# q as two float32r pieces in place of three bf16 pieces, with five record buffers in place of six

## The chip, the core and the metric

The kernel runs on one core of a Trainium2 chip. The core has five engines that run on their own instruction streams: PE (TensorE, matrix products; its weight loads are listed apart as PEld), DVE (VectorE), ACT (ScalarE), POOL (GpSimd) and SP (SyncE, which here only issues transfers). Transfers run on 16 DMA engines. The time is device time of one execution in microseconds, and lower is better. Three executions took 5041.39, 5045.82 and 5046.07 us, a median of 5045.82.

## What is computed

One graph-attention layer over 12,500 nodes with 128 features and 412,500 edges with 64 features, with a residual and two layer norms:

```python
h, q, k, v = x @ Wn + bn, x @ Wq + bq, x @ Wk + bk, x @ Wv + bv
attn_in = concatenate([q[src], k[tgt], edge @ We + be], axis=-1)
hmid = leaky_relu(attn_in @ A1 + b1, 0.2)
scores = leaky_relu(hmid @ A2 + b2, 0.2)
w = softmax(scores.mean(axis=-1), axis=0)          # over all edges
out = segment_sum(w[:, None] * v[tgt], src, num_nodes)
x = layernorm(x + gamma * norm(h + out) + beta)
```

The edges come sorted by tgt (dst). The first layer is linear in its three parts, so q and k already carry their part of A1: the hidden value of an edge is q'[src] + k'[dst] + e'.

## The kernel before

Nodes are laid out as 128 partitions times 98 blocks (nb). Edges come in 403 groups of 8 tiles of 128 edges, sorted by dst. The groups are cut into six parts (CUTS) of 51, 62, 73, 73, 73 and 71 groups.

**Production (`make`, lines 784 to 1009).** For each group, PE multiplies one-hots of dst with rows of the kv table and adds the edge term (`rows`, L901 and L907) into `pkv`; ACT copies two tiles by two into a record buffer `rec` and appends the local src (`evacuate`, L918 and L919); POOL sends each tile's 128 records with an indirect DMA to the place in `rtab` that belongs to the src block (L930). So each record buffer holds four tiles: one ACT copy writes it, four scatters read it, and it is free again when they have landed. `rp = pool("rec", 6)` at L746 has six of them. DVE makes the one-hots (L823, L844), the counts (L834) and the places (L870, L881).

**Sums (`sums_of`, lines 1027 to 1352).** A unit is two src blocks of one part, 49 units a part and 294 in all, each with 14 tiles (four parts), 12 or 10 tiles. A unit's steps are:

- `load` (L1064, SP) brings the unit's records into `rt`, 1820 KB for 14 tiles, and `load_q` (L1075) brings q's pieces of its blocks into `qs`;
- `sources` (L1086, DVE) takes the src column out of `rt`, `turn` (L1094, PE) and `turned` (L1101, DVE) transpose it, `put` (L1108, SP) writes the few bytes to DRAM as `row`, `spread` (L1113, SP) reads them back to all partitions as `rowB`;
- `onehot` (L1122, DVE) compares `rowB` with the partition number and gives `ohT`, for four tiles (512 columns) at a time;
- `hidden` (PE) transposes the k + e part of the four tiles into `ph` (L1133) and adds q of the edge's src by products of q's pieces with `ohT` (L1142), once for each piece;
- `sloped` (L1153, ACT) and `leaky` (L1157, DVE) make the leaky relu `hm`; `scores`, `above_zero` and `heads` give the score (L1170, L1184, L1196), `weights` its exponential (L1235);
- `select` (L1244, DVE) and `weigh` (L1258, ACT) make one-hots times weights, `add` (L1287, PE) sums the v part into `psm`, `total` (L1303, DVE) adds the parts so far, `store` (L1310, SP) writes them.

The steps of eight or so units overlap by a plan that is written out by hand (`do(step, ...)`, eight steps a unit of 14 tiles). At the end of `sorted_path` the loop over parts (from L1608) interleaves the production of part p with the sums of part p-1 in program order; every engine and SP's queue then work strictly in that order. The last part's sums follow after the last group, and `closing` adds the norms in 14 groups of seven blocks.

**Tables (`tables`, from L1535).** During the first part's production, 13 further chunks of the kv table and then 14 chunks of q and h are computed. `parts3` (L1523) cuts a float32 value into three bf16 pieces: a copy by ACT (L1526), a subtraction by DVE (L1531), a copy, a subtraction, a copy. The pieces of q go to `qtab` in DRAM (L1582).

What the code relies on in the products of L1142: a one-hot column picks one row of q, so each piece's product is exact, and three bf16 pieces added up give q back.

Of the kernel before, what the change touches and what calls it, by code (L numbers as in the profile page):

```python
# [9 lines left out]

FP = mybir.dt.float32
BF = mybir.dt.bfloat16
I32 = mybir.dt.int32
U8 = mybir.dt.uint8
AF = mybir.ActivationFunctionType
ALU = mybir.AluOpType
# [4 lines left out]
P = 128  # L21
D = 128
# [4 lines left out]
NB = 7  # L27
# [64 lines left out]
def general(  # L92
# [20 lines left out]

    srcI = const.tile([P, T], I32)
    nc.sync.dma_start(out=srcI, in_=src)

    nc.vector.tensor_scalar(srcI, srcI, rows - 1, None, op0=ALU.min)
    dstI = const.tile([P, T], I32)
    nc.sync.dma_start(out=dstI, in_=dst)
# [155 lines left out]
    with tc.tile_pool(name="gvg", bufs=3) as vp, tc.tile_pool(  # L275
# [7 lines left out]
        def front(g):  # L283
# [30 lines left out]
            )  # L314
            idx = ip.tile([P, GT], I32)
            nc.vector.tensor_tensor(idx, mv, srcF[:, cols], op=ALU.add)
# [136 lines left out]
def sorted_path(  # L453
# [8 lines left out]
    nc = tc.nc  # L462
    nb = plan.nb
# [4 lines left out]

    const = ctx.enter_context(tc.tile_pool(name="const", bufs=1))
    dram = ctx.enter_context(tc.tile_pool(name="dram", bufs=1, space=DRAM))  # L470
    qtab = dram.tile([P, nb, 3 * D], BF, name="qtab")
    kvtab = dram.tile([nb * P, 6 * D], BF, name="kvtab")
    htab = dram.tile([P, nb, D], FP, name="htab")
    xtab = dram.tile([P, nb, D], FP, name="xtab")
# [2 lines left out]
    dtab = dram.tile([G, EG], U8, name="dtab")  # L477
    stab = dram.tile([G, 1], I32, name="stab")

    ident = const.tile([P, P], FP)  # L480
    make_identity(nc, ident)
    identB = const.tile([P, P], BF)
    nc.vector.tensor_copy(identB, ident)
    iotaE = const.tile([P, P, 4], BF)
    nc.gpsimd.iota(iotaE, pattern=[[1, P], [0, 4]], base=0, channel_multiplier=0,
# [21 lines left out]
    for j, part in enumerate((1.0, -1.0)):  # L507
# [13 lines left out]
        out=signs, in_=signs, compare_op=ALU.not_equal, fill=SLOPE - 1, base=-(H + 2),  # L521
# [57 lines left out]
    pool = lambda name, bufs, **k: work.enter_context(tc.tile_pool(name=name, bufs=bufs, **k))  # L579
# [7 lines left out]
    def kv_product(xt, pool, j):  # L587
        pn = pool.tile([P, 4 * P], FP, name="ph")
        nc.tensor.matmul(
            pn[:, : 2 * D], xt[:, j, :], Wkv.rearrange("k s d -> k (s d)"), start=True, stop=True  # L590
        )
        return pn

    def kv_biased(ns, j, pn):
        nc.vector.tensor_add(
            ns[:, j, :, :], pn[:, : 2 * D].rearrange("p (s d) -> p s d", s=2), bias_kv
        )

    def kv_rows(c):

        return kvtab[c * NB * P : (c + 1) * NB * P, :].rearrange("(p b) w -> p (b w)", p=P)

    with tc.tile_pool(name="prep", bufs=1) as prep, tc.tile_pool(
        name="pprep", bufs=1, space=PSUM
# [8 lines left out]
        ns = prep.tile([P, NB, 2, D], FP, name="ns")  # L613
        for j in range(NB):
            kv_biased(ns, j, kv_product(xt, pnode, j))
        skv = prep.tile([P, NB, 3, 2, D], BF, name="skv")
        rest = ns
# [13 lines left out]
    nc.vector.memset(bad, -1.0)  # L631
    blk = const.tile([P, T], BF)
    srcl = const.tile([P, T], U8)
    twin = const.tile([P, T], U8)
    start = const.tile([1, G], I32)
    chunks = [(0, min(CH, G))] + [
# [5 lines left out]
    def edges(tmp, c, size):  # L642

        g0, g1 = chunks[c]
        m = g1 - g0
        dI = tmp.tile([size, EG], I32, name="dI")
        nc.sync.dma_start(out=dI[:m, :], in_=dst_g[g0:g1, :])
# [60 lines left out]
    def spans():  # L708
# [24 lines left out]
        out=above, in_=above, compare_op=ALU.is_gt, fill=0.0, base=0,  # L733
# [9 lines left out]
    kvp = pool("kvs", 5)  # L743
    lp = pool("plc", 2)
    ixp = pool("idx", 6)
    rp = pool("rec", 6)  # L746
    pkvp = pool("pkv", 1, space=PSUM)
    pcp = pool("pcn", 1, space=PSUM)

    qp = pool("qs", 3)  # L750
    slp = pool("sl", 7)
    rowp = pool("row", 2)
    op_ = pool("oht", 3)
# [273 lines left out]
    def sums_of(bp):  # L1027
# [43 lines left out]

        def load_q(i):
            bs = units[i][1]
            qs = qp.tile([P, 2, 3, D], BF, name="qs")
            nc.sync.dma_start(  # L1075
                out=qs[:, : len(bs), :, :].rearrange("p b s d -> p b (s d)"),
                in_=qtab[:, bs[0] : bs[-1] + 1, :],
            )
            state[i]["qs"] = qs
# [38 lines left out]

        def onehot(i, t0, n, k):
            st = state[i]  # L1120
            st["oh"][k] = op_.tile([P, 4 * P], BF, name="ohT")
            nc.vector.tensor_scalar(  # L1122
                st["oh"][k][:, : n * P], st["rowB"][:, t0 * P : (t0 + n) * P], iotaP, None,
                op0=ALU.is_equal,
            )


        def hidden(i, t0, c, n, k):
            st = state[i]
            oh = st["oh"].pop(k)  # L1130
            ph = php.tile([D, 4 * P], FP, name="ph")
            for j in range(n):
                nc.tensor.matmul(  # L1133
                    ph[:, j * P : (j + 1) * P], st["rt"][:, t0 + j, :D], ident,
                    is_transpose=True, start=(j == 0), stop=False,
                )
            t, j0 = units[i][2], t0
            while j0 < t0 + n:
                j1 = min(t0 + n, (j0 // t + 1) * t)
                cols = slice((j0 - t0) * P, (j1 - t0) * P)  # L1140
                for s in range(3):
                    nc.tensor.matmul(  # L1142
                        ph[:, cols], st["qs"][:, j0 // t, s, :], oh[:, cols], start=False,
                        stop=(s == 2 and j1 == t0 + n),
                    )
                j0 = j1
            if c == 0:
                st["hm"][t0 - c] = hp.tile([D, TM * P], FP, name="hm")
            st["ph", k] = ph
# [164 lines left out]
        for i, (nt, nk, s0, load_at, f, e, turn_at) in enumerate(plans):  # L1314
# [4 lines left out]
            do(s0 - turn_at + 1 + e, put, i)  # L1319
            do(s0 - turn_at + 3 + 2 * e, spread, i)  # L1320
            do(s0 - 9, load_q, i)
            for k in range(nk):
                c = 4 * k
                n, s = min(4, nt - c), s0 + 2 * k
# [14 lines left out]
            for j, t0 in enumerate(range(0, nt, 4)):  # L1339
                n = min(4, nt - t0)  # L1340
# [182 lines left out]
    def parts3(to, rest, half):  # L1523

        for s in range(3):
            nc.scalar.activation(to[s], rest, AF.Copy)  # L1526
            yield
            if s < 2:
                less = np_.tile([P, NB, 2, D], FP, name=f"less{s}")
                less = less[:, :, :half, :]  # L1530
                nc.vector.tensor_tensor(less, rest, to[s], op=ALU.subtract)  # L1531
                rest = less
                yield

    def tables():  # L1535
        jobs = [(True, c) for c in range(1, ng)] + [(False, g) for g in range(ng)]
        xts = {}

        def load_x(i):
            if i < len(jobs):  # L1540
                kv, g = jobs[i]
                xts[i] = xp.tile([D, NB, P], FP, name="xt")
                nc.sync.dma_start(
                    out=xts[i], in_=xN[:, g, :, :] if kv else xT[:, g * NB : (g + 1) * NB, :]
                )

        load_x(0)
        yield
        for i, (kv, g) in enumerate(jobs):
            load_x(i + 1)  # L1550
            xt = xts.pop(i)
            ns = np_.tile([P, NB, 2, D], FP, name=f"ns{i % 2}")
            w, bias = (Wkv, bias_kv) if kv else (Wqh, bias_qh)
            for j in range(NB + 1):
                before = ph if j else None
                if j < NB:
                    ph = php.tile([P, 4 * P], FP, name="ph")
                    nc.tensor.matmul(
                        ph[:, : 2 * D], xt[:, j, :], w.rearrange("k s d -> k (s d)"),
                        start=True, stop=True,  # L1560
                    )
                if j:
                    nc.vector.tensor_tensor(
                        ns[:, j - 1, :, :].rearrange("p s d -> p (s d)"), before[:, : 2 * D],
                        bias.rearrange("p s d -> p (s d)"), op=ALU.add,
                    )
                yield
            sp = np_.tile([P, NB, 3, 2, D], BF, name="sp")
            if kv:
                yield from parts3([sp[:, :, s, :, :] for s in range(3)], ns, 2)  # L1570
                nc.sync.dma_start(
                    out=kv_rows(g), in_=sp.rearrange("p b s t d -> p (b s t d)")
                )
                made_rows[0] = g + 1
            else:
                sq = sp.rearrange("p b s t d -> p (b s t d)")[:, : NB * 3 * D].rearrange(
                    "p (b s o d) -> p b s o d", b=NB, s=3, o=1
                )
                yield from parts3([sq[:, :, s, :, :] for s in range(3)], ns[:, :, 0:1, :], 1)
                bl = slice(g * NB, (g + 1) * NB)  # L1580
                nc.sync.dma_start(out=htab[:, bl, :], in_=ns[:, :, 1, :])
                nc.sync.dma_start(  # L1582
                    out=qtab[:, bl, :], in_=sq.rearrange("p b s o d -> p b (s o d)")
                )
            yield
# [147 lines left out]
```

## Time and profile before

| | |
|---|---|
| median of three executions | 5045.82 us |
| the profiled execution, its own time | 5048.47 us |
| its span, first to last instruction | 5046.7 us |
| mean granted TensorE clock | 0.909 |
| PE busy | 4086.8 us (81%), 31,427 records |
| weight loads busy | 3042.3 us (60%), 31,870 records |
| DVE busy | 4082.6 us (81%) |
| ACT busy | 3271.6 us (65%) |
| POOL busy | 3318.5 us (66%) |
| moved by DMA | 1505.35 MB, 298 GB/s on average |

How to read the profile: a group's row names line, engine, operation and tiles (out<-in), the count, its busy time, the mean length of one in ns, then the idle time of that engine just before and what ended it. A row of waits names who waited for whom, the total, how many times and the longest. A row of the timeline has start, length, engine, line, tiles and count. Ends of matmul records are modelled, so distances between starts say more than lengths, and a few per cent of the matmul records are missing. POOL's indirect DMA instruction is the making of the transfer's descriptors; the transfer itself lands later.

### The profile page before, as it was taken

Reading aid. Unit: us, or ns where it says so; the run is one execution under the profiler, and the core shown is the slowest. Engines: PE = TensorE matmul, PEld = TensorE weight load, DVE = VectorE, ACT = ScalarE, POOL = GpSimd, SP = SyncE. Lnnn points to the kernel's source line nnn. Section 1 sums busy time; section 2 is a strip of 40 time slices with the busy share of each in tenths; the row PEclk is TensorE's granted clock in tenths of the full one; section 3 lists DMA queues with packets and bytes.
Section 4 is the critical chain, followed back from the end, with each engine's and each line's share of the span. In section 5 each row is a group of like instructions: output and inputs, shape, how many; then the busy total and the mean of one; then the engine's idle time right before and its main releaser. Section 6 shows DMA issues by size and latency. Waiting matters only on the chain.

```text
span 5046.7 us, 95840 instructions
## 1 busy us (share of the span) xinstructions
PE 4086.8 (81%) x31427; PEld 3042.3 (60%) x31870; DVE 4082.6 (81%) x9078; ACT 3271.6 (65%) x8487; POOL 3318.5 (66%) x3267
## 2 busy tenths in 40 slices
PE   3566667888888888898889899989899999888980
PEld 2333445566666665676667676666676667667760
DVE  7888867778888887888888898888798889666668
ACT  2443345566666666677767777777677777777886
POOL 3777777677777777777777777777777777310002
PEclk6777678899999999999999999999999999999995
DMA  5899889998899988899989899889898999787763
GB/s 179 306 314 354 302 276 335 335 313 292 296 327 329 338 304 288 285 324 318 310 301 316 291 326 317 313 308 311 299 318 311 323 315 325 259 283 271 252 230 140
DMA packets 616624, 1505.35 MB, mean 298 GB/s; under 512 B 104462, under 2 KB 329889, under 8 KB 614324
## 3 DMA queue, kind: packets, MB, share of 16 engines
q1 hardware_dynamic: 461024, 1069.73, 64.1%
q0 software_dynamic: 154752, 429.39, 22.3%
q8 instruction: 253, 4.15, 0.3%
q14 instruction: 255, 2.09, 0.1%
q10 hardware_dynamic: 340, 0.01, 0.0%
HBM read 929.49 MB, written 608.37 MB: 305 GB/s over the span
## 4 chain that ended last, share of the span: by engine, by line
DMA 39%; DVE 24%; PE 11%; POOL 9%; ACT 8%; issue 7%; SPq 1%; DVEq 0%; ACTq 0%; POOLq 0%
DMA rtab<-rec,idx 16%; POOL rtab L930 9%; DMA row<-slT 8%; DMA rt<-rtab 6%; DMA rowB<-row 6%; DVE ohd L844 3%; DVE hm L1157 3%; ACT ohw L1258 3%; PE psm L1287 2%; DVE few L834 2%; ACT rec L918 2%; DVE pos L881 2%; PE pkv L907 2%; DVE ohT L1122 2%; PE psc L1170 1%
## 5 line engine op out<-in xcount | busy, mean ns | idle before, releaser
L930 POOL DMA_INDIRECT rtab<-rec,idx x3224 | 3256.1, 1010 | 1086.1 <-issue 790.7
L918 ACT ACTIVATE rec<-pkv 128x1024 f32<-128x1024 f32 x806 | 822.0, 1020 | 1029.0 <-PE pkv L907 620.2
L1258 ACT ACTIVATE ohw<-ohs,w 128x128 f32<-128x128 bf16 x3822 | 1261.1, 399 | 203.2 <-DVE ohs L1244 84.6
L1287 PE MATMUL psm<-rt,ohw 128*128 128x128 f32 x7644 | 1113.4, 288 | 0.6 <-ACT ohw L1258 0.6
L1287 PEld LDWEIGHTS psm<-rt,ohw 128*128 128x128 f32 x7644 | 985.5, 198 | 75.9 <-ACT hm L1153 10.1
L1157 DVE TENSOR_TENSOR hm<-ph,hm 128x512 f32<-128x512 f32 (+1 forms) x1078 | 669.9, 621 | 271.3 <-ACT hm L1153 263.5
L1133 PE MATMUL ph<-ident,rt 128*128 128x128 f32 x3822 | 648.1, 288 | 154.3 <-DVE hm L1157 150.5
L1142 PE MATMUL ph<-ohT,qs 128*128 128x512 bf16 (+3 forms) x3673 | 719.4, 312 | 35.5 <-DVE ohT L1122 8.9
L901 PE MATMUL pkv<-kvs,ohd 128*128 128x256 bf16 x3224 | 528.7, 290 | 174.2 <-ACT rec L918 153.3
L1133 PEld LDWEIGHTS ph<-ident,rt 128*128 128x128 f32 x3822 | 423.0, 145 | 382.5 <-issue 180.0
L907 PE MATMUL pkv<-WeS,eat 64*128 64x128 f32 x6448 | 626.1, 317 | 0.0
L1122 DVE TENSOR_SCALAR ohT<-rowB,iotaP 128x512 bf16<-128x512 uint8 (+1 forms) x1078 | 499.5, 463 | 152.3 <-DMA rowB<-row 152.1
L1153 ACT ACTIVATE hm<-ph 128x512 f32<-128x512 f32 (+1 forms) x1078 | 577.8, 536 | 57.2 <-PE ph L1142 47.1
L907 PEld LDWEIGHTS pkv<-WeS,eat 64*128 64x128 f32 x6448 | 462.4, 202 | 189.7 <-issue 183.9
L844 DVE TENSOR_SCALAR ohd<-dstb,node 128x1152 bf16<-128x1152 uint8 x404 | 564.9, 1399 | 4.3 <-DMA dstb<-dtab 4.3
L901 PEld LDWEIGHTS <-ohd 128*128 128x128 bf16 x3224 | 314.5, 104 | 379.2 <-issue 289.5
L1142 PEld LDWEIGHTS <-qs 128*128 128x128 bf16 x4116 | 394.8, 99 | 140.6 <-issue 18.6
L1244 DVE TENSOR_TENSOR ohs<-iotaE,sl 128x512 bf16<-128x512 bf16 (+1 forms) x1078 | 419.1, 389 | 4.2 <-ACT ohw L1258 4.2
L834 DVE TENSOR_REDUCE few<-oh 128x99 bf16<-128x792 bf16 x403 | 395.1, 980 | 13.9
L870 DVE TENSOR_TENSOR ats<-pc,oh 128x792 f32<-128x792 f32 x403 | 391.2, 971 | 16.5 <-PE pc L852 16.1
L881 DVE TENSOR_REDUCE pos<-ats 128x8 f32<-128x792 f32 x403 | 389.6, 967 | 1.7
L1170 PE MATMUL psc<-hm,A2s 128*32 128x512 f32 (+3 forms) x2352 | 343.3, 552 | 55.4 <-DVE slT L1101 52.4
(157 smaller groups left out, 3700.6 us busy)
## 6 DMA issues: line engine op xcount, KB each, us to landing
rt<-rtab SPq DMA_DIRECT2D x196, 1820.0 KB
eat<-in_ea SPq DMA_DIRECT2D x201, 512.0 KB
rt<-rtab SPq DMA_DIRECT2D x49, 1560.0 KB
rt<-rtab SPq DMA_DIRECT2D x49, 1300.0 KB
qs<-qtab SPq DMA_DIRECT2D x294, 192.0 KB
rtab<-rec,idx POOLq DMA_INDIRECT x3224
dstb<-dtab SPq DMA_DIRECT2D x201, 256.0 KB
rtab<-empty SPq DMA_DIRECT2D x98, 520.0 KB
```

The costliest lines, as they stand in the source:

```text
L844: nc.vector.tensor_scalar(to, ids[:, cols], node, None, op0=ALU.is_equal)
L901: nc.tensor.matmul(pk[:, h, i, :], ohd[t], kvs, start=(i == 0), stop=False,)
L907: nc.tensor.matmul(pk[:, h, i, :D], eat[h * DE : (h + 1) * DE, (j + i) * P : (j + i + 1) * P], WeS[h * DE : (h + 1) * DE, :], start=False, ...
L918: nc.scalar.activation(rec[:, :, :, : 2 * D], pk, AF.Copy)
L930: one_tile = nc.gpsimd.indirect_dma_start(out=rtab[p % TABS][:, :], out_offset=bass.IndirectOffsetOnAxis(ap=idxs[g][:, t : t + 1], axis=0) ...
L1122: nc.vector.tensor_scalar(st["oh"][k][:, : n * P], st["rowB"][:, t0 * P : (t0 + n) * P], iotaP, None, op0=ALU.is_equal,)
L1133: nc.tensor.matmul(ph[:, j * P : (j + 1) * P], st["rt"][:, t0 + j, :D], ident, is_transpose=True, start=(j == 0), stop=False,)
L1142: nc.tensor.matmul(ph[:, cols], st["qs"][:, j0 // t, s, :], oh[:, cols], start=False, stop=(s == 2 and j1 == t0 + n),)
L1153: nc.scalar.activation(hm, state[i]["ph", k][:, : n * P], AF.Copy, scale=SLOPE)
L1157: nc.vector.tensor_tensor(hm, ph[:, : n * P], hm, op=ALU.max)
L1258: nc.scalar.activation(ohw[:, j, :], ohs[:, :, j], AF.Copy, scale=st["w"][:, t0 + j : t0 + j + 1])
L1287: nc.tensor.matmul(st["psS"][:, (1 + u) * P : (2 + u) * P], ohw[:, j, :], st["rt"][:, t0 + j, D : 2 * D], start=(k == 0), stop=(k == t - 1),)
```

## The change

- `qtab` and `qs` hold two pieces of four bytes in place of three of two bytes: 1,024 bytes a node in place of 768. `qs` is declared float32r.
- the one-hot `ohT` is written as float32r, four bytes an element in place of two.
- the products of L1142 run over two pieces. In the changed program they bring their own weights; before, each had a weight load as an instruction of its own.
- `parts2` takes the place of `parts3` for q: ACT rounds q to float32r, DVE subtracts that from q, and the remainder is the second piece as it is. It yields as often as `parts3` did, so the work around it keeps its order.
- `rp` has five record buffers. The other edits take 4,608 bytes more a partition (three `qs` buffers of 512 bytes and three `ohT` buffers of 1,024 bytes more); a record buffer is 4,160 bytes.

The order of all other instructions (but for the copies of the tables) on each engine and on SP's and POOL's queues stays as it was.

```diff
+FR = mybir.dt.float32r
...
-    qtab = dram.tile([P, nb, 3 * D], BF, name="qtab")
+    qtab = dram.tile([P, nb, 2 * D], FP, name="qtab")
...
-    rp = pool("rec", 6)
+    rp = pool("rec", 5)
...
-            qs = qp.tile([P, 2, 3, D], BF, name="qs")
+            qs = qp.tile([P, 2, 2, D], FR, name="qs")
             nc.sync.dma_start(
-                out=qs[:, : len(bs), :, :].rearrange("p b s d -> p b (s d)"),
+                out=qs[:, : len(bs), :, :].rearrange("p b s d -> p b (s d)").bitcast(FP),
                 in_=qtab[:, bs[0] : bs[-1] + 1, :],
             )
...
-            st["oh"][k] = op_.tile([P, 4 * P], BF, name="ohT")
+            st["oh"][k] = op_.tile([P, 4 * P], FR, name="ohT")
...
-                for s in range(3):
+                for s in range(2):
                     nc.tensor.matmul(
                         ph[:, cols], st["qs"][:, j0 // t, s, :], oh[:, cols], start=False,
-                        stop=(s == 2 and j1 == t0 + n),
+                        stop=(s == 1 and j1 == t0 + n),
                     )
...
+    def parts2(to, q):
+
+        yield
+        nc.scalar.activation(to[:, :, 0, :, :].bitcast(FR), q, AF.Copy)
+        yield
+        yield
+        nc.vector.tensor_tensor(to[:, :, 1, :, :], q, to[:, :, 0, :, :], op=ALU.subtract)
+        yield
+        yield
...
-                sq = sp.rearrange("p b s t d -> p (b s t d)")[:, : NB * 3 * D].rearrange(
-                    "p (b s o d) -> p b s o d", b=NB, s=3, o=1
-                )
-                yield from parts3([sq[:, :, s, :, :] for s in range(3)], ns[:, :, 0:1, :], 1)
+                sq = sp.rearrange("p b s t d -> p (b s t d)").bitcast(FP)[
+                    :, : NB * 2 * D
+                ].rearrange("p (b s o d) -> p b s o d", b=NB, s=2, o=1)
+                yield from parts2(sq, ns[:, :, 0:1, :])
```

## The prediction

> **What bounds the kernel now.** I read the page first, then the busy time by stage, the waits of POOL, of ACT and of SP's queue, the chain of waits of the last stage, and single units in the timeline.
>
> ```profile
> span 5046.7 us, 95840 instructions
> DMA 39%; DVE 24%; PE 11%; POOL 9%; ACT 8%; issue 7%; SPq 1%; DVEq 0%; ACTq 0%; POOLq 0%
> 65.00:560.00 495.00, 294.97 (x1467) 188.98 (x1468) 411.01 (x649) 191.19 (x247) 377.68 (x340) 0.71 0.95 321
> 560.00:1110.00 550.00, 411.73 (x3042) 293.44 (x3072) 401.35 (x834) 287.09 (x728) 398.95 (x403) 0.83 0.89 309
> 1110.00:4345.00 3235.00, 2869.42 (x23018) 2152.80 (x23377) 2761.79 (x5915) 2274.01 (x6041) 2478.77 (x2482) 0.96 0.90 310
> 4345.00:4850.00 505.00, 445.70 (x3443) 354.46 (x3490) 311.15 (x925) 382.61 (x1100) 31.23 (x15) 0.98 0.78 266
> 4850.00:4904.00 54.00, 50.74 (x405) 41.94 (x408) 33.80 (x108) 47.26 (x143) 0.00 (x0) 1.00 0.52 169
> ```
>
> The window rows give, after the length, busy time and count of PE, weight loads, DVE, ACT and POOL, then granted clock, DMA share and GB/s. The chain spreads over everything, so shares settle nothing; POOL looks idle a quarter of the time. Its own row over 3,230 us of the middle says otherwise:
>
> ```profile
> L930 POOL DMA_INDIRECT rtab<-rec,idx x2478 | 2476.4, 999 | 755.3 <-issue 606.2 <-DMA rtab<-rec,idx 35.4 <-ACT ohw L1258 32.6
> POOL rtab L930 <- ACT rec L919: 22.0, 18, 4.0
> ACT rec L918 <- DMA rtab<-rec,idx: 319.4, 160, 4.1
> ```
>
> Busy 2476.4 and idle 755.3 make 3231.7: the idle time is 2478 times 0.305 us, the cadence between two scatters, and nothing else. A scatter costs 0.999 + 0.305 = 1.30 us, eight of them a group, and POOL never waits for data. ACT waits for POOL instead: 160 times a record buffer was not yet free. So from 1110 to 4345 us POOL sets the pace and the rest has slack. The second row (window 560 to 1110 us) is the one stretch where POOL starves: 22.0 us in 18 waits, 16.5 without the cadence.
>
> After the last scatter, 49 units of part 5 remain (4345 to 4904 us), then 143 us of closing, which the change doesn't touch. What the units wait for:
>
> ```profile
> by line: DMA row<-slT 32.5%; DMA rowB<-row 29.8%; DVE hm L1157 5.0%; PE psm L1287 4.7%; DVE ohT L1122 4.1%; PE ph L1142 3.6%; PE ph L1133 3.3%; DMA rt<-rtab 2.9%; ACT ohw L1258 1.9%; PE psc L1170 1.9%; DVE ohs L1244 1.7%; DVE slT L1101 1.6%
> SPq L1113 <- DMA row<-slT: 174.5, 50, 5.5
> SPq L1064 <- PE psm L1287: 14.8, 22, 1.4
> 4714.75 0.32 SPq L1113 DMA_DIRECT2D rowB<-row  x1
> 4715.77 0.37 SPq L1064 DMA_DIRECT2D rt<-rtab  x1
> 4719.77 0.33 SPq L1108 DMA_DIRECT2D row<-slT  x1
> 4720.15 0.46 SPq L1075 DMA_DIRECT2D qs<-qtab  x1
> 4724.99 0.32 SPq L1113 DMA_DIRECT2D rowB<-row  x1
> ```
>
> This is a ring of transfers: SP issues rt (1.8 MB), row queues behind it, SP stands until row has landed, issues rowB, then the next rt. One turn here is 10.24 us. PE enters it only where rt waits for a buffer that PE frees: 14.8 us in 22 waits.
>
> **The change part by part.** *Products over q.* Three bf16 pieces become two float32r pieces: 4,116 products with as many separate weight loads become 2,744 products that bring their own weights.
>
> ```profile
> 4664.30 0.81 PE L1142 MATMUL ph<-ohT,qs 128*128 128x512 bf16 x3
> 4667.14 0.49 PE L1142 MATMUL ph<-ohT,qs 128*128 128x256 bf16 x3
> 4667.47 1.06 PE L1287 MATMUL psm<-rt,ohw 128*128 128x128 f32 x8
> 4651.72 1.06 PE L1170 MATMUL psc<-hm,A2s 128*32 128x512 f32 x8
> L1142 PE MATMUL ph<-ohT,qs 128*128 128x512 bf16 x100 | 28.1, 379 | 1.0
> L1142 PE MATMUL ph<-ohT,qs 128*128 128x256 bf16 x57 | 9.3, 273 | 0.0
> L1170 PE MATMUL psc<-hm,A2s 128*32 128x512 f32 x120 | 21.2, 605 | 0.0
> L1287 PE MATMUL psm<-rt,ohw 128*128 128x128 f32 x545 | 74.8, 277 | 0.0
> ```
>
> From first start to last end, less one product's length, by the count less one: (0.81 - 0.379)/2 = 0.216 us from one 512-column bf16 product to the next, (0.49 - 0.273)/2 = 0.109 for 256, so 0.42 ns a column. A unit of 14 tiles has chunks of 512, 384 + 128, 512 and 256 columns, 1792 in all, three times over: 2.26 us. No row shows float32r; the neighbours bound it. Below: bf16's 0.42 ns. Above: an f32 pass. L1170's eight records are two passes of four products that run side by side, (1.06 - 0.605) = 0.45 us from pass to pass, 0.86 ns a column. I take the lower one. An f32 product shows as two records (7,644 at L1287 for 3,822 tiles), each at twice bf16's time per column: four column-times, which fits two halves of one operand times two halves of the other. A type that keeps one piece of each needs one of the four. A floor remains: L1287's f32 passes of 128 columns follow each other by (1.06 - 0.277)/7 = 0.112 us, however short, which I read as the weight load; it applies to the 128-column products (two at 0.112 for three at 0.054) and to the 256 ones. New sum: 4 x 0.216 + 2 x 0.162 + 2 x 0.112 + 2 x 0.112 = 1.63 us, 0.63 us less a unit. At the f32 rate: 2 x 1792 x 0.86 ns = 3.08 us, 0.82 us more.
>
> The Trainium skill's FP8 and Floating Point Precision (TensorE Precision Notes) says the same of the passes: reduced-precision FP32 is read as four bytes and cut to 22 bits, true FP32 is four passes. By it the sum stays at 1.63 us a unit; no run here shows it yet.
>
> Before 4345 us the saved PE time is hidden under POOL: zero (in the starved stretch anything from -17 to +10, since more bytes go there too; between them I take 0). In the ring it can only shorten the 14.8 us of rt's waits, each about as long as the saving: -8 (0 to -15). From 4850 to 4904 us PE is busy 50.7 of 54 us and drains four units: 4 x 0.63 = -2.5.
>
> *One subtraction less for each of 14 q tables* (and two ACT copies, which nobody on POOL's path waits for).
>
> ```profile
> 478.36 1.09 DVE L1531 TENSOR_TENSOR less<-less,sp 128x896 f32<-128x896 f32 x1 [1.02 <-ACT sp L1526]
> 478.48 1.80 POOL L930 DMA_INDIRECT rtab<-rec,idx  x1 [0.31 <-ACT sp L1526]
> L1531 DVE TENSOR_TENSOR less<-less,sp 128x896 f32<-128x896 f32 x12 | 13.0, 1085 | 3.0 <-ACT sp L1526 3.0
> L1531 DVE TENSOR_TENSOR less<-ns,sp 128x896 f32<-128x896 f32 x11 | 12.0, 1090 | 9.5 <-ACT sp L1526 9.5
> L930 POOL DMA_INDIRECT rtab<-rec,idx x154 | 161.8, 1051 | 48.9 <-issue 38.7 <-DMA rtab<-rec,idx 2.6 <-ACT rec L919 2.4
> ```
>
> A scatter that starts inside such a subtraction ends when the subtraction has ended plus its own 0.96 us: 1.80 instead of 0.96. From 345 to 555 us, where 23 of them lie, a scatter takes 1.051 us against 0.999 later: 154 x 0.052 = 8 us, 0.35 each. POOL is the bound there, so 14 x 0.35 = -5 (0 to 14 x 0.84 = -12).
>
> *More bytes.* qs grows from 192 to 256 KB for each of 294 units, the table's writes from 14 x 672 to 14 x 896 KB.
>
> ```profile
> 4398.00:4612.00 214.00, 183.71 (x1418) 145.60 (x1436) 131.32 (x377) 157.93 (x456) 28.42 (x13) 0.99 0.84 287
> 4704.00:4849.00 145.00, 135.85 (x1073) 108.53 (x1081) 91.71 (x283) 119.65 (x343) 0.00 (x0) 1.00 0.72 248
> L1113 SPq DMA_DIRECT2D rowB<-row x19: 319/320/327, 4398.4 to 4601.5; - x19
> L1113 SPq DMA_DIRECT2D rowB<-row x15: 319/320/320, 4704.5 to 4848.8; - x15
> ```
>
> A turn of the ring takes 203.1/18 = 11.28 us while 287 GB/s move and 144.3/14 = 10.31 at 248 GB/s: 3.24 against 2.56 MB a turn, 1.4 us for each further MB. 65.5 kB more would be 0.09 us, over 49 units +4.6. But qs is issued while SP waits for row and is in no one's way until rowB starts; I take +2 (0 to +4.6). The table's 3.2 MB at 321 GB/s are 10 us of transfers in a stage whose DMA share is 0.95, but POOL waits there only 2.6 us for landings, most of it cadence: +1 (0 to +10). In the POOL-bound middle the bytes are hidden, as long as POOL's row keeps its 0.305 us.
>
> *The one-hot in four bytes* (L1122) at 0: an f32 tensor_scalar takes no longer than the bf16 one.
>
> ```profile
> L1122 DVE TENSOR_SCALAR ohT<-rowB,iotaP 128x512 bf16<-128x512 uint8 x833 | 409.8, 492 | 152.3 <-DMA rowB<-row 152.1
> L677 DVE TENSOR_SCALAR q<-q 128x416 f32<-128x416 f32 x5 | 1.9, 377 | 0.2
> L677 DVE TENSOR_SCALAR q<-q 128x832 f32<-128x832 f32 x1 | 0.6, 584 | 0.0
> ```
>
> Half a ns an element between 416 and 832 gives 425 ns at 512. Were the mode lost, another 0.25 us for each of 833.
>
> *Five record buffers.* One buffer is four scatters, 5.2 us of lead of ACT over POOL. ACT will stand longer for a buffer, and consumers' ACT work queues behind it, but all of it ahead of POOL: 0 (up to +21, once a buffer's worth after each of the four part changes).
>
> Sum: -8 - 2.5 - 5 + 2 + 1 = -12.5 us on this execution's span of 5046.7 (its time 5048.5, 2.7 above the runs' median 5045.82): 5033 as a median.
>
> **The rivals.**
> *Hidden anyway* (5046): the ring's turns are set by rt and row; SP's wait on PE becomes a wait for row, and qs adds its bytes. For it: 174.5 us of waits on row against 14.8 on PE. It keeps within 8 us of before.
> *float32r streams at the f32 rate* (slower, 5090): 0.82 us more a unit. The place is the last production part, where PE is at 0.9 and POOL's margin is smallest:
>
> ```profile
> 0.00:1110.00 1110.00, 210.59 (x373) 776.63 (x743) 0.76 0.89 302
> 1110.00:3702.00 2592.00, 571.02 (x998) 1985.23 (x1991) 0.96 0.90 309
> ```
>
> These count the instructions on rec, two of ACT a record and four of POOL: (373 + 998)/2 - (743 + 1991)/4 = 2.0 records of lead at 3702 us. About 46 units still come in production there: 46 x 0.82 = 38 less 10 us of lead: +27; the ring takes half of 49 x 0.82: +20; the drain +3; less 5. It decides from 0.33 us for 512 columns, where two pieces cost what three do. The Trainium skill's SBUF — State Buffer (SBUF: two separate sides) gives TensorE's port 614 GB/s; by that 128 x 512 x 4 bytes take 0.43 us, this rival's rate. The f32 rows agree with it, but they don't tell a port from a split operand.
> *It isn't one pass at all* (the change doesn't do what it says): two records each as in f32, 6.2 us a unit in place of 2.26, where a production unit of 15.5 us (73 groups at 10.4 us over 49 units) has 1.7 us of PE to spare (PE at 0.89): 2.2 us x 245 and more, above 5500. Against it: each tile's type is asked for by name in the products.
> *The one-hot loses its mode*: 0.9 us of DVE a unit, with DVE at 0.85: about 5085.
> *The buffer bites*: POOL starves after part changes, up to +21 on the sum: 5054. Against it: 2.0 records of lead at the worst point.
> *More than forecast* (5009): the starved stretch closes (-17) and rt never waits for PE (-7 more). For it: PE is at 0.75 in that stretch, at a clock of 0.83; against it: the DMA share of 0.89.
>
> **How the numbers follow.** Forecast 0.50 (5018 to 5044: 0.37 faster, 0.13 within), hidden 0.17 (within), more 0.07 (faster), f32 rate 0.14, not one pass 0.03, one-hot 0.04 (slower), buffer 0.05 (0.03 within, 0.02 slower). A change under 0.2%, 10 us, is about what a measurement of this kernel can't tell from none. Faster 0.44, same 0.33, slower 0.23. The range runs from 5005 to 5090, which leaves out the two-pass case and the outer halves of the slower ones; the forecast's own is 5018 to 5044.
>
> **What would show it.** Right: L1142's 512-column products 0.22 us apart, one record each, in a PE busy time about 180 us lower; L930 still cadence only from 1110 to 4340 us, its last scatter near 4340; ring turns of 10 to 11 us; ACT's waits for rec longer than 319 us. Wrong: products 0.4 us apart, POOL's idle row naming ACT rec, L1122 above 0.5 us, or turns longer by more than 0.1 us.

## The result, and the profile after

The changed kernel takes 5052.67 us (median of 20 executions, 5046.57 to 5061.86) against 5045.62 for the kernel before in the same rounds (20 executions, 5034.35 to 5054.06). The ratio is 1.0015, with a 95% interval of 1.0009 to 1.0021: about 7 us slower, where 12 us faster was forecast. That is under 0.2%, but its interval lies wholly on the slower side. The profiled execution took 5061.86 us, 9 more than its median; single executions of one kernel differ by as much as the whole effect, so a stage of one profile can be read only where it differs by much more than a few us, or in the same way in several kernels.

Busy time by stage, after (window, length, then PE, weight loads, DVE, ACT and POOL, granted clock, DMA share, GB/s), for the windows shown of before:

```profile
65.00:560.00 495.00, 286.85 (x1451) 184.00 (x1453) 393.00 (x626) 168.38 (x221) 364.73 (x333) 0.71 0.94 320
560.00:1110.00 550.00, 407.19 (x2967) 295.70 (x2968) 402.89 (x843) 282.45 (x723) 403.15 (x410) 0.84 0.92 319
1110.00:4345.00 3235.00, 2829.95 (x22324) 2188.46 (x22323) 2757.64 (x5903) 2264.76 (x6023) 2479.29 (x2477) 0.95 0.91 314
4345.00:4850.00 505.00, 427.15 (x3235) 359.35 (x3234) 304.46 (x912) 377.80 (x1092) 36.73 (x20) 0.97 0.78 268
4850.00:4904.00 54.00, 48.55 (x387) 41.79 (x386) 35.51 (x106) 45.14 (x131) 0.00 (x0) 1.00 0.54 181
```

POOL starts 333 scatters up to 560 us where it started 340, and the windows after that hold 410 for 403, then 2477 for 2482: seven fall behind in the first part, come back in the starved stretch, and five fall behind later. PE's busy time fell by 60.8 us in all (4086.8 to 4026.0), not by 180.

The group of POOL, after, and the waits of ACT, after and before, all from 1110 to 4340 us:

```profile
L931 POOL DMA_INDIRECT rtab<-rec,idx x2473 | 2476.7, 1002 | 754.6 <-issue 605.7 <-DMA rtab<-rec,idx 37.7 <-ACT ohw L1259 30.2
```

```profile
ACT rec L919 <- DMA rtab<-rec,idx: 392.5, 182, 6.2
ACT rec L918 <- DMA rtab<-rec,idx: 310.9, 157, 4.1
```

POOL's idle time is still 0.305 us a scatter and nothing else, so this stage is bound as before; ACT waits for a record buffer 182 times in place of 157 (the 160 waits of the prediction are those of the whole execution). That is what five buffers were expected to show.

The table stage is another matter. POOL's group from 345 to 555 us, after (before: 154 scatters, 1051 ns, 48.9 us idle):

```profile
L931 POOL DMA_INDIRECT rtab<-rec,idx x149 | 151.5, 1017 | 60.0 <-issue 36.3 <-ACT rec L920 15.5 <-DMA rtab<-rec,idx 5.2
```

A scatter became 34 ns shorter, 5 us over 149 of them, which is the size that was forecast for one subtraction less. But POOL's waits beyond the cadence grew from 48.9 - 154 x 0.305 = 1.9 us to 60.0 - 149 x 0.305 = 14.6 us, and they are now waits for the record that ACT should have filled.

The products over q, in PE's timeline of one unit after (start, length, line, shape, count):

```profile
4658.81 0.48 PE L1143 MATMUL ph<-ohT,qs 128*128 128x256 f32 x2
4659.13 1.05 PE L1288 MATMUL psm<-rt,ohw 128*128 128x128 f32 x8
...
4661.73 0.71 PE L1143 MATMUL ph<-ohT,qs 128*128 128x512 f32 x2
4662.27 0.38 PE L1218 MATMUL psm<-ident,mx 128*128 128x128 f32 x2
...
4664.88 0.77 PE L1143 MATMUL ph<-ohT,qs 128*128 128x384 f32 x4
4665.48 0.66 PE L1288 MATMUL psm<-rt,ohw 128*128 128x128 f32 x4
```

and three rows of before that the prediction does not show:

```profile
4662.64 0.82 PE L1142 MATMUL ph<-ohT,qs 128*128 128x384 bf16 x6
4663.30 0.66 PE L1287 MATMUL psm<-rt,ohw 128*128 128x128 f32 x4
...
4664.94 1.05 PE L1287 MATMUL psm<-rt,ohw 128*128 128x128 f32 x8
```

From the start of a chunk's products to the start of what follows: 512 columns 0.54 us (4662.27 - 4661.73) where three bf16 products took 0.64; 384 and 128 together 0.60 for 0.66; 256 columns 0.32 for 0.33. A unit of 14 tiles takes 2 x 0.54 + 0.60 + 0.32 = 2.00 us in place of 2.27. It is one record a product, as forecast, and far from the 0.86 ns a column of an f32 pass, but two products take 0.27 us each for 512 columns, not 0.216.

The tail: waits of SP's queue from 4345 to 4904 us, after, and the count of the spreads with the first and last start (after, then before).

```profile
SPq L1114 <- DMA row<-slT: 178.6, 50, 6.4
...
SPq L1065 <- PE psm L1288: 11.6, 24, 2.1
```

```profile
L1114 SPq DMA_DIRECT2D rowB<-row x47: 319/320/327, 4396.1 to 4889.0; - x47
```

```profile
L1113 SPq DMA_DIRECT2D rowB<-row x46: 319/320/327, 4398.4 to 4875.2; - x46
```

SP's waits on PE for a buffer of rt are 11.6 us in this execution where they were 14.8; in a second profile of the changed kernel (`e18_after_again`) they are 17.0. From the last spread to the end of the span it is 5060.1 - 4889.0 = 171.1 us after and 5046.7 - 4875.2 = 171.5 before: the drain is 0.4 us shorter, not 2.5.

### The profile page after: what moved, and what is told of

The parts are those of the page before. It is cut to its first block, busy times and chain, and to the rows that moved or that the text cites. A ratio compares the mean times of both kernels' runs of the same rounds, so it can differ in the third digit from the quotient of the medians.

```text
span 5060.1 us, 93546 instructions
## 1 busy us (share of the span) xinstructions
PE 4026.0 (80%) x30498; PEld 3090.5 (61%) x30498; DVE 4064.0 (80%) x9064; ACT 3240.4 (64%) x8459; POOL 3315.7 (66%) x3267
## 4 chain that ended last, share of the span: by engine, by line
DMA 38%; DVE 21%; PE 11%; ACT 11%; POOL 10%; issue 8%; SPq 1%; DVEq 0%; ACTq 0%; POOLq 0%
DMA rtab<-rec,idx 15%; POOL rtab L931 10%; DMA row<-slT 8%; DMA rowB<-row 6%; DMA rt<-rtab 5%; ACT ohw L1259 4%; DVE ohd L845 3%; DVE hm L1158 3%; ACT rec L919 3%; PE psm L1288 2%; DVE few L835 2%; PE pkv L908 2%; ACT hm L1154 2%; DVE pos L882 2%; PE pkv L902 2%
## 5 line engine op out<-in xcount | busy, mean ns | idle before, releaser
L1288 PE MATMUL psm<-rt,ohw 128*128 128x128 f32 x7644 | 1145.2, 293 | 0.6 <-ACT ohw L1259 0.6
L1288 PEld LDWEIGHTS psm<-rt,ohw 128*128 128x128 f32 x7644 | 1018.0, 203 | 71.6 <-ACT hm L1154 16.6
L1143 PE MATMUL ph<-ohT,qs 128*128 128x512 f32 (+3 forms) x2744 | 750.9, 373 | 12.7 <-DVE ohT L1123 12.4
L1123 DVE TENSOR_SCALAR ohT<-rowB,iotaP 128x512 fp32r<-128x512 uint8 (+1 forms) x1078 | 497.9, 462 | 167.9 <-DMA rowB<-row 167.1
L902 PEld LDWEIGHTS <-ohd 128*128 128x128 bf16 x3224 | 303.1, 104 | 420.9 <-issue 351.1
L1143 PEld LDWEIGHTS ph<-ohT,qs 128*128 128x128 f32 x2744 | 430.4, 196 | 17.2 <-DVE ohT L1123 17.2
```

What stands on the lines that cost most here:

```text
L902: nc.tensor.matmul(pk[:, h, i, :], ohd[t], kvs, start=(i == 0), stop=False,)
L1123: nc.vector.tensor_scalar(st["oh"][k][:, : n * P], st["rowB"][:, t0 * P : (t0 + n) * P], iotaP, None, op0=ALU.is_equal,)
L1143: nc.tensor.matmul(ph[:, cols], st["qs"][:, j0 // t, s, :], oh[:, cols], start=False, stop=(s == 1 and j1 == t0 + n),)
L1288: nc.tensor.matmul(st["psS"][:, (1 + u) * P : (2 + u) * P], ohw[:, j, :], st["rt"][:, t0 + j, D : 2 * D], start=(k == 0), stop=(k == t - 1),)
```

## The experiments

Theories at the start: A, the bytes (q's pieces take a third more in `qs` and in the table); B, the record buffer; C, the float32r products themselves. The kernel before was timed beside each of them, on the same chip in the same rounds; every ratio below is to that, with its 95% interval.

**First four runs: a chip on which nothing of this shows.** Five buffers, four buffers, the bytes alone, and the changed kernel again.

```diff
e1_rec5 (and e7, e9)      e2_rec4
-    rp = pool("rec", 6)  -    rp = pool("rec", 6)
+    rp = pool("rec", 5)  +    rp = pool("rec", 4)
```

```diff
e3_bytes (and e11)
-    qtab = dram.tile([P, nb, 3 * D], BF, name="qtab")
+    qtab = dram.tile([P, nb, 4 * D], BF, name="qtab")
...
-    rp = pool("rec", 6)
+    rp = pool("rec", 5)
...
-            qs = qp.tile([P, 2, 3, D], BF, name="qs")
+            qs = qp.tile([P, 2, 4, D], BF, name="qs")
...
+                nc.scalar.activation(sq[:, :, 3, :, :], ns[:, :, 0:1, :], AF.Copy)
```

> The kernel before with five record buffers in place of six, nothing else. Measured so far: the change as a whole makes the kernel 7 us slower (ratio 1.0015, 1.0009 to 1.0021). Theory A (bytes: qs and the q table carry a third more bytes, in the ring of the tail and in the starved stretch): the buffer costs nothing, ratio 1.0000 within 0.0006. Theory B (the buffer: ACT's lead over POOL falls from about 20 to 15 us, so POOL starves more often before 1110 us and after part changes): +5 to +10 us, ratio 1.0010 to 1.0020, more gaps on POOL than the 42 us of before, and the ring's turns in the tail unchanged at 10.70 us.

> The kernel before with four record buffers: the suspected cost of one buffer doubled. Theory A: still nothing or little, under +5 us, as long as the lead after part changes (4.1 us at its least with six buffers) is not used up. Theory B: at least twice the cost of one buffer, +12 to +40 us, ratio 1.0024 to 1.008, with POOL's gaps above 60 us.

> The kernel before with five record buffers and q held in four bf16 pieces of which three are multiplied: qs 256 KB a unit and the table 14 x 896 KB, as in the changed kernel, with the bf16 products and both subtractions of before (and 14 ACT copies more). Theory A: +5 to +8 us over the kernel with five buffers alone, and about +0.1 us in each of the 49 turns of the ring (10.70 to about 10.83 us). Theory B: the same time as with five buffers alone. Theory C (the float32r products themselves, with their slower weight loads or the lower clock): neither this nor the buffer shows a cost; both come out within 2 us of before.

> The changed kernel once more, for a second profile beside the first and for times next to those of the parts. Ratio 1.0009 to 1.0021 as measured. What is a property of the kernel and not of one execution shows again: last scatter about 5 to 8 us later than 4345 us, turns of the ring of 10.8 us, POOL's gaps about 50 us.

The kernel before took 6021.86 us here. Ratios: 0.9996 (0.9986 to 1.0006), 1.0006 (0.9995 to 1.0017), 1.0000 (0.9988 to 1.0011), and for the changed kernel 0.9963 (0.9950 to 0.9975), faster by 22 us. The page of the run with five buffers, its chain of waits by engine, and POOL's group from 1110 to 4345 us:

```profile
PE 38%; DVE 14%; issue 13%; DMA 10%; ACT 10%; another core or an unknown queue 9%; POOL 5%; SPq 0%; ACTq 0%; DVEq 0%; POOLq 0%
```

```profile
L930 POOL DMA_INDIRECT rtab<-rec,idx x1982 | 1956.9, 987 | 1279.0 <-issue 500.8 <-ACT rec L919 390.1 <-ACT w L1235 169.1
```

PE has 38% of the chain (11% before), and POOL is idle for 1279 us, 674 more than its cadence, waiting for ACT's records. The granted clock is 0.845 against 0.909. By these rows PE sets the pace here, POOL waits for it through ACT, and the change gains. These runs don't answer for a chip on which POOL sets the pace, as it does in the profile before. On a second chip of this kind (before 6018.72 us) five buffers again (`e7_rec5`) came to 1.0004 (0.9994 to 1.0014), and the bytes alone again (`e8_bytes`, 1.001 to 1.002 if the bytes cost where POOL sets the pace) to 0.9993 (0.9981 to 1.0005).

**One product and three.** From here on POOL sets the pace again (the kernel before takes 5046 to 5065 us) unless it is said.

```diff
e5_one (from the kernel after)       e6_three
-                for s in range(2):  -                for s in range(2):
+                for s in range(1):  +                for r, s in enumerate((0, 1, 1)):
```

> The changed kernel with one float32r product a tile in place of two (the low piece of q is left out of the sum; all bytes, buffers and DVE work stay): PE is relieved by about another 1 us a unit. Where POOL's scatters set the pace (kernel before at about 5045 us): theory A and B say that PE's time is hidden, so no more than 5 us under the changed kernel, ratio to before 1.000 to 1.002; theory C says that the float32r products cost it, so 7 us or more under it, ratio at or below 1.000. Where the chip grants less clock and PE sets the pace (kernel before at about 6020 us, as in the first four runs): the ratio falls well below the 0.9963 of the changed kernel, to about 0.96 (294 units, 1 us each over the 0.845 clock, near 300 us would be 0.95).

> The changed kernel with three float32r products a tile (the low piece is added twice): PE is loaded by about another 1 us a unit over the changed kernel, some 0.75 us a unit over before. Where POOL sets the pace: theories A and B say at most 10 us over the changed kernel, unless PE then becomes the bound near 4340 us, where the lead is least; theory C says 7 us or more on top of the changed kernel for each product, ratio above 1.003. Where PE sets the pace (6020 us): +250 to +300 us, ratio about 1.04.

Before: 5059.75 us. One product 1.0021 (1.0011 to 1.0031), three 1.0020 (1.0009 to 1.0031). Half the products or half as many again, and the time is the same within some 7 us: PE's time is worth nothing that shows on this chip, in production or in the ring, and theory C is out. Both kernels have the bytes and the buffer of the change.

**The buffer alone**, where POOL sets the pace.

> The kernel before with five record buffers, a third time, still for a chip on which POOL's scatters set the pace (kernel before near 5050 us). Theory B (the buffer): ratio 1.001 to 1.002, POOL's gaps beyond its cadence 55 to 65 us instead of 42, most of them before 1250 us, last scatter 8 to 15 us later. Theory A (bytes and the rest): ratio 1.0000 within 0.0006, gaps of about 42 us. Where PE sets the pace (6020 us): ratio 1.000 again.

1.0001 (0.9990 to 1.0011). Theory B is out, as far as 5 us.

**The bytes taken away.** The one product of `e5_one`, with only its piece stored and loaded.

```diff
e10_half (from e5_one)
-    qtab = dram.tile([P, nb, 2 * D], FP, name="qtab")
+    qtab = dram.tile([P, nb, D], FP, name="qtab")
...
-            qs = qp.tile([P, 2, 2, D], FR, name="qs")
+            qs = qp.tile([P, 2, 1, D], FR, name="qs")
...
-                ].rearrange("p (b s o d) -> p b s o d", b=NB, s=2, o=1)
+                ].rearrange("p (s b o d) -> p b s o d", b=NB, s=2, o=1)
...
-                    out=qtab[:, bl, :], in_=sq.rearrange("p b s o d -> p b (s o d)")
+                    out=qtab[:, bl, :], in_=sq[:, :, 0, :, :].rearrange("p b o d -> p b (o d)")
```

> The changed kernel with one float32r product a tile, as in the run with one product, and now the low piece is not stored or loaded either: qs 128 KB a unit in place of 256, the table 14 x 448 KB in place of 14 x 896 (the low piece is computed and left out of the sum). It differs from the run with one product (ratio 1.0021, 1.0011 to 1.0031) in bytes alone. The buffer has come out at 1.0001 (0.9990 to 1.0011) by itself, so theory B is nearly out. Theory A (bytes): twice what the change added is taken away, so 12 to 20 us less, ratio 0.998 to 0.9995. Theory D (neither bytes nor buffer nor PE: the order of the work in the starved stretch, or float32r itself): ratio 1.001 to 1.003 as with one product. Where PE sets the pace (6020 us): 0.95 to 0.98 by the product left out.

0.9979 (0.9970 to 0.9989): 0.0042 or 21 us below the same kernel with 256 KB, which ran on another chip (each against the kernel before beside it). Theory A holds, theory D does not.

**Where the bytes cost.** `qs` 256 KB again for the last part's units, or for all others (a load fetches the neighbours' rows too), or the low piece written to a table that nobody reads, in 14 transfers more.

```diff
e12_tail, e14_tail (from e10_half); e13_prod, e15_prod with "< NP - 1"
+            w = len(bs) * (2 if units[i][0] == NP - 1 else 1)
+            b0 = min(bs[0], nb - w)
...
-                in_=qtab[:, bs[0] : bs[-1] + 1, :],
+                in_=qtab[:, b0 : b0 + w, :],
```

```diff
e16_tables (from e10_half)
+                nc.sync.dma_start(
+                    out=qlow[:, bl, :], in_=sq[:, :, 1, :, :].rearrange("p b o d -> p b (o d)")
+                )
```

> The kernel with one float32r piece stored, loaded and multiplied (qs 128 KB; ratio to before 0.9979, 0.9970 to 0.9989), with qs 256 KB again for the 49 units of the last part alone, those of the ring after the last scatter (a load fetches its neighbours' rows too). Theory A1 (the bytes cost in the ring, 1.4 us for each further MB of a turn, 49 x 131 kB = 6.4 MB): +9 us, ratio 0.9997. Theory A2 (they cost where POOL starves, before 1250 us, or wherever scatters set the pace): ratio 0.998 as without them.

> The same kernel with qs 256 KB for the 245 units of the first five parts alone, which run under the scatters (the table's writes stay 14 x 448 KB). Theory A1: no cost, ratio 0.998. Theory A2: the 32 MB bring back most of the 21 us between the runs with 256 and 128 KB, +8 to +20 us, ratio 0.9995 to 1.002; if not, the table's writes (6.4 MB less in the stage with a DMA share of 1.0) are what is left.

These two met a chip where PE sets the pace (before 6100.38 us): 0.9926 (0.9911 to 0.9942) and 0.9919 (0.9901 to 0.9938), the gain of the product left out, and no answer. Again, with 5064.80 us for before:

> As in the run before it of this name (qs 256 KB for the 49 units of the last part alone, 128 KB for the others), for a chip on which POOL's scatters set the pace (kernel before near 5050 us). Theory A1 (the bytes cost in the ring): +9 us on the ratio of 0.9979 without them, 0.9997. Theory A2 (they cost in production): 0.998.

> As in the run before it of this name (qs 256 KB for the 245 units that run under the scatters, 128 KB in the ring, the table's writes 14 x 448 KB), for a chip on which POOL sets the pace. Theory A1: 0.998. Theory A2: 0.9995 to 1.002, with the last scatter 8 to 20 us later than the 4341 of the run with 128 KB throughout; if it stays at 0.998 as well, the table's writes are left.

Tail 0.9996 (0.9987 to 1.0005), production 0.9990 (0.9981 to 0.9999): 9 and 6 us over 0.9979, each with some 7 us of uncertainty, as both intervals count. Production's 6 us by itself is therefore not clear of nothing.

> The kernel with one float32r piece (qs 128 KB throughout, 0.9979), which now writes the low piece too, into a table of its own that nobody reads: the writes of the starved stage are 14 x 896 KB again, as in the changed kernel, in 28 transfers. If the bytes cost wherever they are moved, the writes are worth what is left of 21 us after the ring (0.9996) and production (0.9990): about 7 us, ratio 0.999 to 0.9995. If they are hidden, 0.998, and the three places don't add up.

1.0004 (0.9995 to 1.0013), 13 us over 0.9979. The writes cost; that they cost the most of the three is not shown, as the three differ by no more than their errors. Whether it is their bytes or their number (28 transfers in place of 14) this run does not tell apart. The three places together give 27 us where the whole was 21: within their errors they add up.

**Without the subtraction.**

```diff
e17_single (from e10_half)
-        nc.vector.tensor_tensor(to[:, :, 1, :, :], q, to[:, :, 0, :, :], op=ALU.subtract)
```

> The kernel with one float32r piece, 128 KB, and without the 14 subtractions that computed the low piece: q is stored as its float32r rounding alone. Against 0.9979 with them it prices a subtraction in the stage where POOL is the bound: the prediction's 0.35 us each gives -5 us, ratio 0.997; if DVE's subtractions cost POOL nothing, 0.998. Below both kernels in either case.

0.9985 (0.9976 to 0.9994), against 0.9979 with the subtractions: they are worth nothing that shows, and by the two intervals no more than some 4 us. This kernel keeps q as its float32r rounding alone, the low piece is left out of the sum; where POOL sets the pace, it and `e10_half` are the fastest that ran, 8 to 11 us under the kernel before. The run with its table written in full (`e16_tables`) was timed beside it on one chip: 5046.63 us against 5037.41, 9 us more with 448 KB more a write and the 14 subtractions.

**The bytes alone, beside the change.**

> The kernel before with five record buffers and q in four bf16 pieces of which three are multiplied: the change's bytes (qs 256 KB, table 14 x 896 KB) with the products, weight loads and subtractions of before, and 14 ACT copies more. If the bytes are the whole cost: 7 to 12 us over before, ratio 1.0014 to 1.0024, where POOL sets the pace. If float32r or the new order in the table stage has a part in it: 1.000 to 1.001.

> The changed kernel again, beside the bytes alone. Where POOL sets the pace 1.0009 to 1.0021 as before, and within 5 us of the kernel with the bytes alone: PE's saving and the subtraction less are then worth nothing that shows. A kernel well under the bytes alone (6 us or more) would give the saving a value.

Before 5059.44 us: the bytes alone, with bf16 products and both subtractions, 1.0027 (1.0016 to 1.0038); the changed kernel 1.0023 (1.0011 to 1.0036). The bytes by themselves (with 14 ACT copies more) cost about what the change costs.

**The place in the profile.** POOL's group from 450 to 650 us, one row each: before, after, the half of the bytes, its table written in full, the bytes alone.

```profile
L930 POOL DMA_INDIRECT rtab<-rec,idx x149 | 153.0, 1027 | 47.7 <-issue 37.2 <-ACT rec L919 4.1 <-DMA rtab<-rec,idx 3.0
```

```profile
L931 POOL DMA_INDIRECT rtab<-rec,idx x142 | 144.0, 1014 | 57.0 <-issue 34.8 <-ACT rec L920 16.5 <-DMA rtab<-rec,idx 3.4
```

```profile
L931 POOL DMA_INDIRECT rtab<-rec,idx x150 | 154.3, 1029 | 45.7 <-issue 38.4 <-DMA rtab<-rec,idx 4.0 <-DVE ohd L845 1.2
```

```profile
L932 POOL DMA_INDIRECT rtab<-rec,idx x144 | 144.2, 1001 | 56.8 <-issue 36.0 <-ACT rec L921 8.6 <-DVE sp L1543 6.4
```

```profile
L930 POOL DMA_INDIRECT rtab<-rec,idx x142 | 146.8, 1034 | 54.3 <-issue 36.0 <-ACT rec L919 9.0 <-DVE ats L870 4.2
```

The count falls as the bytes of a table's write grow, in every kernel that ran where POOL sets the pace, and the time from the start of the first of the 14 writes to the start of the last grows with them:

| bytes of q in one of the 14 writes | kernels | scatters, 450 to 650 us | first to last write, us | ratio |
|---|---|---|---|---|
| 448 KB | half; no subtraction; tail; production | 150; 153; 152; 151 | 230; 230; 231; 233 | 0.9979; 0.9985; 0.9996; 0.9990 |
| 672 KB | before; five buffers | 149; 148 | 241; 243 | 1; 1.0001 |
| 2 x 448 KB | table written in full | 144 | 244 | 1.0004 |
| 896 KB | after; after again; one product; three; bytes alone | 142 in all five | 246; 247; 247; 248; 255 | 1.0015; 1.0023; 1.0021; 1.0020; 1.0027 |

The writes themselves, before, after, and with half the bytes:

```profile
L1582 SPq DMA_DIRECT2D qtab<-sp x14: 325/420/3681, 350.0 to 591.0; - x14
L1593 SPq DMA_DIRECT2D qtab<-sp x14: 326/2212/4696, 352.2 to 598.4; - x14
L1593 SPq DMA_DIRECT2D qtab<-sp x14: 325/2352/4825, 346.6 to 576.6; - x14
```

And the stage from 450 to 560 us, after, and with half the bytes:

```profile
450.00:560.00 110.00, 65.29 (x340) 42.00 (x340) 81.02 (x140) 27.59 (x46) 74.44 (x73) 0.74 1.02 359
```

```profile
450.00:560.00 110.00, 68.09 (x354) 43.84 (x356) 87.10 (x154) 29.55 (x49) 85.34 (x81) 0.74 1.03 357
```

357 and 359 GB/s with a DMA share over 1.0: the transfers are full in both, and what differs is how much has to pass. From half the bytes to the changed kernel, 13 x 448 KB more pass between the first and the last write: 6.0 MB, an estimate of 17 us at 359 GB/s, and the stage is 16 us longer. POOL makes up part of that: it is 8 scatters behind at 560 us (333 against 341), 8 x 1.30 = 10 us.

What of this reaches the end is seen in one pair of profiles alone. With the table written in full, 404 scatters have started by 650 us and 744 by 1110, against 413 and 752 without the subtraction, and the last scatter ends 11 us later (4341.5 against 4330.1). Before and after are not such a pair: there the seven scatters lost by 560 us are made up by 1110.

## Why the prediction was wrong, point by point

**The steps that failed.** Two did. The larger: the savings of -8, -2.5 and -5 were taken to reach the end of the kernel, and the runs show nothing of them (one product or three: 1.0021 and 1.0020; without the subtractions 0.9985 against 0.9979). That alone turns the sum from -12.5 to +3. The other: the bytes were put at +3 and cost 10 to 13, which is the rest of the miss. The rival "hidden anyway" had the mechanism of the first step and, with "qs adds its bytes" and its 8 us, the size; it had a chance of 0.17.

**The table's writes**, "+1 (0 to +10)", were taken near the lower end because "POOL waits there only 2.6 us for landings". That was the wrong row. POOL's wait for landings stays short after the change (5.2 us); what grows is its idle time beyond the cadence, from 1.9 to 14.6 us between 345 and 555, put down to ACT's records there and to ACT and DVE in the other kernels of 896 KB. I read that as late transfers that hold up the inputs of the next group; no run separates it. The row that decides was in the same paragraph: a DMA share of 0.95 over the stage (1.04 before from 450 to 560 us). The stage grew by about what the bytes take at the full rate. The price at the end is less sure: half of the 13 us of the full table, or of the 9 us on one chip, is +5 to +6 for the change's 3.2 MB, where +1 was taken. The Trainium skill's DMA: Bandwidth & Descriptors (Specifications) gives about 358 GB/s as the limit between HBM and one core; the 357 and 359 GB/s of the two rows above, and 362 before in the same window, agree with it.

**The other bytes.** "+2 (0 to +4.6)" for qs in the ring and nothing in production. Half of what the runs put on 128 KB is +4 and +3 for the change's 64 KB, each uncertain by about as much. The ring's upper bound may have been the price too, but no profile shows it: a turn takes 10.60 us before and 10.72 after by the spreads above, 10.72 with five buffers alone (before's bytes), 10.70 with the change's bytes alone and 10.80 with half. All bytes together: 10 to 13 us (half of 21, or 1.0027 against 1.0001), where +3 was taken.

**-8 and -2.5 for PE's time.** PE's own time went the way that was forecast, by less than forecast. The term assumed 0.216 us for a float32r product; the second product starts 0.31 us after the first, and the unit saves 0.27 us in place of 0.63. The weight load of a float32r product takes 191 ns where bf16's takes 98 (rows below, 4400 to 4850 us). That the second product stands behind its own load is my reading: in the chunk at 4661.73 its load ends at 4662.00 and it starts at 4662.04.

```profile
L1143 PEld LDWEIGHTS ph<-ohT,qs 128*128 128x128 f32 x417 | 65.3, 191 | 0.0
```

```profile
L1142 PEld LDWEIGHTS <-qs 128*128 128x128 bf16 x630 | 60.0, 98 | 20.7 <-issue 0.3
```

The Trainium skill's TensorE: Matmul & The Clock Gate (Weight-path perf modes) says that fast weight load is off for FP32 inputs; these rows agree for float32r in so far as its 191 ns are those of the f32 loads of `add` (195 ns after; those of the transposes in `hidden` take 142), not bf16's 98. The port's rate in the Trainium skill's SBUF — State Buffer (SBUF: two separate sides), by which the prediction had 0.43 us a product as a rival, is not borne out: 0.54 us for two. And what was saved bought nothing that shows: one product or three give 1.0021 and 1.0020. The -8 stood on SP's waits on PE in the ring getting shorter as PE is relieved. They don't: 14.8 us before, 11.6 and 17.0 in two profiles of the changed kernel, 19.8 with one product, 20.0 with three. The waits for row are 174.5 to 183.2 us in the same profiles (all from 4345 to 4904 us). That fits a ring that is set by its transfers, the rival "hidden anyway".

**-5 for the subtractions.** The size was right where it was measured (1051 to 1017 ns a scatter), the step from there to the end was not: the stage is held by transfers, and POOL's shorter scatters wait longer. Without the last 14 subtractions POOL is busy 155.4 us from 345 to 555 in place of 160.8, and idle 55.2 in place of 50.9; the time did not gain (0.9985 against 0.9979). A slip of reading beside it: the scatter at 478.48 ends 0.83 us after the subtraction, not 0.96.

**0 for the buffer and 0 for the one-hot** were right: 1.0001 (0.9990 to 1.0011), and 490 ns for 512 elements after (492 before):

```profile
L1123 DVE TENSOR_SCALAR ohT<-rowB,iotaP 128x512 fp32r<-128x512 uint8 x833 | 408.0, 490 | 167.9 <-DMA rowB<-row 167.1
```

So the sum -12.5 becomes: PE 0, subtractions 0, bytes +10 to +13, against a measured +7 to +12 (1.0015 and 1.0023). That the bytes are the cause is shown by the runs as a whole (`e9_rec5`, `e10_half`, `e11_bytes`). How their cost divides between the table, the ring and the scatters stays open, and so does why, in the profiled execution after, seven scatters lost by 560 us are made up by 1110 and five lost again by 4345: at 1002 ns a scatter against 999 the later loss is within what executions of the same bytes show (997 to 1002).

## What to carry to other kernels

Before an edit that trades engine time for bytes, look for the stage in which the DMA share is at 1 and estimate every added byte there at the full rate, whoever the busiest engine is and however short its own waits on transfers are; some of it may be made up later, as it was here. A gain measured on the bounding engine's instructions counts only if the stage isn't also full elsewhere. And a saving that is hidden on one chip may be the whole effect on another: measure a change of this size on more than one.

## What the runs showed of the hardware beside that

- The same program takes 5046 to 5065 us on some chips and 6019 to 6100 on others, with the granted TensorE clock at 0.91 and at 0.84 to 0.85. On the slower kind the changed kernel is faster, 0.9963 (0.9950 to 0.9975).
- The granted clock falls as PE gets less to do. On one chip, mean over the executions: three products 0.914, before 0.909, the changed kernel 0.898, one product 0.873. The same 7,644 matmul records of `add` are busy for 1111 us with three products, 1141 in the changed kernel and 1196 with one in the profiles of that chip: part of what an edit saves on PE is taken back by the clock. The Trainium skill's TensorE: Matmul & The Clock Gate (Part 1: The HAM clock gate) says that the clock follows how busy PE has been; these four agree.
